# A slot tile's rows two tiles ahead and behind the weights in SyncE's queue, instead of three ahead and in front of them

## The chip, the cores and the metric

The kernel runs on one core of one Trainium2 chip. The metric is the device time of one execution in microseconds (us). Engines are named as in the profile: PE is TensorE, DVE is VectorE, ACT is ScalarE, POOL is GpSimd, SP is SyncE, which only issues DMAs here.

## What is computed

One pre-norm transformer layer on x of shape (4, 2048, 256), float32: causal linear attention with 16 heads of 16, and then a mixture of 8 experts with the top two per token.

```python
x = x + linear_attention(layernorm(x))      # q, k = elu(.) + 1; running sums of k v and of k over the sequence
h = layernorm(x)                            # 8192 tokens
logits = h @ router_w.T                     # 8 experts
top, idx = top_k(logits, 2);  probs = softmax(top)
hmid = gelu(einsum('th,efh->etf', h, w1) + b1)     # 256 -> 512
y    = einsum('etf,ehf->eth', hmid, w2) + b2       # 512 -> 256
out  = x + einsum('eth,te->th', y, combine)        # combine holds probs at the two chosen experts
```

## The kernel before

**Blocks and iterations.** The 8192 tokens are 16 blocks of 512. The main loop has 18 iterations s. Iteration s runs three stages side by side as generators: stage_a of block s (layernorm, projections, the normalizer), stage_b of block s-1 (attention), stage_c of block s-2 (output projection, layernorm, router). Stage_c ends with two small matmuls on PE (`pc`, L596 and L599) that count how many earlier tokens chose each expert. From these DVE works out a slot for each token and choice, and POOL scatters the normalized rows to the DRAM tensor `rows` with eight indirect DMAs (L624). In `rows` each expert has a region of its own, so 256 consecutive slots belong to one expert.

**Slot tiles.** The expert part works on slot tiles of 256 slots. `ROUNDS` says how many full tiles are sure to exist after a number of blocks, whatever the router chose: 5, 4, 8, 8, 8, 8, 8, 22. When a round opens, `plan(r)` finds on DVE which expert and which first row each tile of the round has, and puts them in a small tile `where`. 68 tiles are run in this way; the last few stand under a condition on a count read at run time.

**What one tile does.** `slot_tiles` is a generator over tiles j; each tile takes two steps.

- fetch_rows(j): SP reads the expert and the row number from `where` into registers (L742, L743) and loads the 256 slot rows into a tile `xs` (L747, three buffers).
- fetch_in(j): SP loads the expert's w1 (L759, three buffers). fetch_out(j): w2 and b2 (L767, L771, three buffers).
- turned(j): PE transposes `xs` (`pt_xs`, L780), DVE copies the result to `xT` (L781) and takes the token numbers and weights from the rows.
- hidden(j): PE's first matmul (`ph`, L808), ACT's gelu (L814).
- output(j): PE's second matmul (`py`, L825), DVE's bias and weights (L830, L834); one tile later POOL adds the rows to the output in DRAM (L839).

The first step of tile j holds hidden(j), turned(j+1), fetch_rows(j+3), fetch_in(j+2); the second holds output(j-1), the store of an older tile and fetch_out(j+1).

**What a slot load waits for.** A load of slot rows depends on the scatters that were recorded before it:

```python
after(i, writes + cleared)        # writes: every scatter recorded so far
```

This list also holds scatters of blocks that the tile does not need.

**The order.** SP's queue is issued in the order in which the program is written (`in_order`, a manual schedule of SP alone); an instruction of SP that waits holds all behind it. The order on PE, DVE, ACT and POOL is set when the kernel is built, by a scheduler that goes by the order of recording and by estimates of when operands are ready; each of these engines then runs its list in order.

**Steps per iteration.** Before each iteration the main loop works out how many steps of slot tiles it may take: `limit = 2 * (open_tiles - 3)`, less the steps taken, shared over the iterations until the next round opens. This gives 4, 4, 4 steps in iterations 5 to 7, 8 in each of 8 to 16 and none in 17; the steps left over run after the loop, where no attention work is left. The steps of an iteration are spread between the steps of the three stages.

Of the kernel before, what the change touches and what calls it, by code (L numbers as in the profile page):

```python
# [9 lines left out]
F32 = mybir.dt.float32  # L10
# [6 lines left out]
P = 128  # L17
# [7 lines left out]
def kernel(  # L25
# [44 lines left out]
    E, _, F = w1.shape  # L70
# [10 lines left out]
    NS = ST // P  # L81
# [10 lines left out]
    R = D + 4  # L92
# [5 lines left out]
    moe = ctx.enter_context(tc.tile_pool(name="moe", bufs=2))  # L98
# [12 lines left out]
    def load_x(n: int):  # L111
        b, s0 = blocks[n]
        xt = att.tile([P, NT, D], F32, tag="x", bufs=4, name=f"x_{n}")
        step = P if n == 0 else TB
        for i in range(0, TB, step):
            nc.scalar.dma_start(
                xt[:, i // P : (i + step) // P, :],
                x[b, s0 + i : s0 + i + step, :].rearrange("(t p) d -> p t d", p=P),
            )
        return xt  # L120

    xs = {0: load_x(0)}
# [97 lines left out]
    def ins_of(i):  # L220
        return getattr(i, "ins", i)
# [6 lines left out]
    def after(inst, others):  # L228
        for o in others:
            tc.add_manual_dep(inst, o.name, AFTER, reason="rows written before")  # L230
# [501 lines left out]
    def slot_tiles(todo):  # L732


        state = {}

        def fetch_rows(j):
            r, k = todo[j]
            if r not in plans:
                plans[r] = plan(r)  # L740
            where, te, b1t, behind = plans[r]
            e = nc.sync.value_load(where[0:1, 0, k : k + 1], min_val=0, max_val=E - 1)  # L742
            row = nc.sync.value_load(  # L743
                where[0:1, 1, k : k + 1], min_val=0, max_val=SPARE
            )
            xs_t = moe.tile([P, NS, R], F32, tag="xs", bufs=3, name=f"xs_{r}_{k}")
            i = ins_of(nc.sync.dma_start(  # L747
                xs_t, rows[ds(row, ST), :].rearrange("(a p) d -> p a d", p=P)
            ))
            tc.add_to_no_dep_group("rows", i)  # L750
            after(i, writes + cleared)
            state[j] = {
                "e": e, "xs": xs_t, "bias": b1t[:, k, :], "te": te[:, k : k + 1],
                "behind": None if behind is None else behind[:, k : k + 1],
            }

        def fetch_in(j):
            w1t = moe.tile([P, NCC, F], F32, tag="w1", bufs=3, name=f"w1_{j}")
            nc.sync.dma_start(  # L759
                w1t, w1[ds(state[j]["e"], 1), :, :].rearrange("o (cc p) f -> p (o cc) f", p=P)  # L760
            )
            state[j]["w1"] = w1t

        def fetch_out(j):
            e = state[j]["e"]
            w2t = moe.tile([P, NFC, D], F32, tag="w2", bufs=3, name=f"w2_{j}")
            nc.sync.dma_start(  # L767
                w2t, w2[ds(e, 1), :, :].rearrange("o (fc p) d -> p (o fc) d", p=P)
            )
            b2t = moe.tile([P, D], F32, tag="b2", bufs=3, name=f"b2_{j}")  # L770
            nc.sync.dma_start(b2t, b2[ds(e, 1), :].to_broadcast([P, D]))  # L771
            state[j]["w2"], state[j]["b2"] = w2t, b2t

        def turned(j):
            xs_t = state[j]["xs"]
            xT = moe.tile([P, NCC, ST], F32, tag="xT", name="xT")
            pt = bank([P, NCC, NS, P], "pt_xs")
            for cc in range(NCC):
                for a in range(NS):
                    nc.tensor.transpose(pt[:, cc, a, :], xs_t[:, a, ts(cc, P)], ident)  # L780
            copied = nc.vector.tensor_copy(  # L781
                xT.rearrange("p c s -> p (c s)"), pt.rearrange("p c a s -> p (c a s)")
            )
            state[j]["xs"] = xT

            to = moe.tile([P, NS], U32, tag="to", bufs=10, name=f"to_{j}")
            follow(nc.vector.tensor_copy(to, xs_t[:, :, D]), copied)
            wt = moe.tile([P, NS], F32, tag="wt", bufs=6, name=f"wt_{j}")
            follow(nc.vector.scalar_tensor_tensor(
                wt, xs_t[:, :, D + 3], state[j]["te"], xs_t[:, :, D + 2],  # L790
                ALU.is_equal, ALU.mult,
            ), copied)
            nc.vector.tensor_tensor(wt, wt, xs_t[:, :, D + 1], ALU.add)
            if state[j]["behind"] is not None:
                nc.vector.scalar_tensor_tensor(
                    wt, token[:, 0:NS], state[j]["behind"], wt, ALU.is_ge, ALU.mult
                )
            state[j]["to"], state[j]["wt"] = to, wt

        def hidden(j):  # L800
            xT, w1t, bias = (state[j][key] for key in ("xs", "w1", "bias"))
            hT = moe.tile([P, NFC, ST], F32, tag="hT", name="hT")
            for f2 in range(NFC // 2):
                ph = bank([P, 2, ST], "ph")
                for i in range(2):
                    f = 2 * f2 + i
                    for cc in range(NCC):
                        nc.tensor.matmul(  # L808
                            ph[:, i, :], w1t[:, cc, ts(f, P)], xT[:, cc, :],
                            start=(cc == 0), stop=(cc == NCC - 1),  # L810
                        )
                for i in range(2):
                    f = 2 * f2 + i
                    nc.scalar.activation(  # L814
                        hT[:, f, :], ph[:, i, :], AF.Gelu, bias=bias[:, f : f + 1]
                    )
            state[j]["hT"] = hT
# [33 lines left out]
            return store  # L851

        J = len(todo)
        LEAD = 3
        for j in range(min(LEAD, J)):
            fetch_rows(j)
            if j < LEAD - 1:
                fetch_in(j)
        fetch_out(0)
        yield  # L860
        turned(0)
        wait = []
        for j in range(J + 1):
            if j < J:
                hidden(j)
            if j + 1 < J:
                turned(j + 1)
            if j + LEAD < J:
                fetch_rows(j + LEAD)
            if j + LEAD - 1 < J:  # L870
                fetch_in(j + LEAD - 1)
            if j < J:
                yield
            if j > 0:
                wait.append(output(j - 1))
            while len(wait) > (j < J):
                wait.pop(0)()
            if j + 1 < J:
                fetch_out(j + 1)
            if j < J:  # L880
                yield

# [5 lines left out]
    class Work:  # L888


        def __init__(self, todo):
            self.todo = todo
            self.it = slot_tiles(todo)
            self.steps = 0
# [13 lines left out]
    open_tiles = 0  # L908
    NBLK = len(blocks)
    clear_rows()  # L910
    for s in range(NBLK + 2):
        gens = []
        if s < NBLK:
            gens.append(stage_a(s))
        if 0 <= s - 1 < NBLK:
            gens.append(stage_b(s - 1))
        if s - 2 >= 0:
            gens.append(stage_c(s - 2))

        limit = 2 * (open_tiles - 3)  # L920
        left = max(0, limit - work.steps)

        upto = min([n + 2 for n in begins if n + 2 >= s])
        if s == NBLK + 1:
            left = max(0, left - 2 * HOLD)
        share = -(-left // (upto - s + 1))
        ran = 0
        order = (20, 12, 5)[(s > NBLK - 1) + (s > NBLK)]
        i = 0
        while gens:  # L930
            for it in list(gens):
                if next(it, "end") == "end":
                    gens.remove(it)
                i += 1
                while ran < share and ran * order < i * share:
                    work.step()
                    ran += 1
        while ran < share:
            work.step()
            ran += 1  # L940
        if s - 2 in begins:
            open_tiles += ROUNDS[begins[s - 2]]
# [4 lines left out]
    with ExitStack() as within:  # L947
        for tile_ in todo[LIKELY:]:
            within.enter_context(tc.If(held > tile_[1]))
            for _ in slot_tiles([tile_]):  # L950
                pass
# [44 lines left out]
```

## Time and profile before

| | |
|---|---|
| time of the runs, median (lowest to highest) | 1150.33 us (1149.88 to 1155.89), 3 runs |
| profiled execution: time, span | 1153.22 us, 1151.3 us |
| mean granted PE clock | 0.956 |
| busy: PE, DVE, ACT, POOL | 1035.5, 761.7, 414.7, 389.6 us |
| slot loads (L747): number, KB, median us from issue to landing | 68, 260, 3.3 |
| w1 and w2 loads: number, KB, median us to landing | 136, 512, 5.5 |
| scatters to `rows` (L624): number, mean POOL time | 128, 0.975 us |

The span is from the first to the last instruction of the profiled execution, and its time is a little longer. Busy times of different engines lie beside each other. The profile's timelines give the start of each instruction in us from the span's start, its length, the engine, the line and the tensors; SPq is SP's queue. In brackets stands how long the engine was idle before, and what released it. Iterations 8 to 14 repeat with a period of 62.2 us and hold four slot tiles each.

### The profile page before, as it was taken

To read this page: it belongs to the slowest core of one execution; us is meant where nothing else is said; L and a number is where in the kernel's file an instruction comes from. 1 tells how busy PE (TensorE), PEld (TensorE's weight loads), DVE (VectorE), ACT (ScalarE), POOL (GpSimd) and SP (SyncE) were. 2 spreads that over 40 slices of the span, in tenths; PEclk is the share of its full clock that TensorE was granted. 3 is DMA by queue.
4 is the path that set the end of the run, shared out by engine and by line. 5 is a ranking of instruction groups with operands and counts; after the bars stand their busy time and mean duration, and the time that the engine had idled before them with its cause. 6 is when DMAs were issued, how large, how long until landed. Compare 5 with 4: busy or idle time off the path is not lost.

```text
span 1151.3 us, 23771 instructions
## 1 busy us (share of the span) xinstructions
PE 1035.5 (90%) x8736; PEld 824.5 (72%) x8736; DVE 761.7 (66%) x2534; ACT 414.7 (36%) x824; POOL 389.6 (34%) x302
## 2 busy tenths in 40 slices
PE   5878777797979999999999999999999889999991
PEld 3556556575757687877778777878788678888881
DVE  8778878777677858776777668775777463333330
ACT  3433342434342625353444435362532212222220
POOL 4003123021315253434232433425142353444444
PEclk9889889988989999999999999999999989999996
DMA  6011121441425356372828273736446549888963
GB/s 203 1 38 39 38 75 59 155 138 47 137 58 156 99 132 181 94 221 54 253 45 242 57 213 83 210 81 167 129 104 192 144 131 304 230 231 231 235 151 37
DMA packets 128726, 155.27 MB, mean 135 GB/s; under 512 B 9952, under 2 KB 105952, under 8 KB 128608
## 3 DMA queue, kind: packets, MB, share of 16 engines
q1 hardware_dynamic: 84944, 101.78, 28.0%
q0 software_dynamic: 25728, 34.88, 16.1%
q10 hardware_dynamic: 17936, 17.07, 4.6%
q8 instruction: 70, 1.15, 0.4%
q14 instruction: 48, 0.39, 0.1%
HBM read 108.05 MB, written 45.65 MB: 134 GB/s over the span
## 4 chain that ended last, share of the span: by engine, by line
PE 66%; DVE 27%; DMA 3%; ACT 2%; issue 2%; ACTq 0%; POOL 0%; DVEq 0%; POOLq 0%
PE py L825 20%; PE ph L808 17%; PE pp L338 7%; DVE at L444 6%; PE pn L467 5%; DVE st L266 4%; PE pv L361 3%; PE sc L439 3%; PE pt_xn L259 2%; PE pn L460 2%; DMA out_dram<-y,to 2%; PE pt_xs L780 2%; DVE x L528 2%; DVE z L348 1%; DVE mv L267 1%
## 5 line engine op out<-in xcount | busy, mean ns | idle before, releaser
L839 POOL DMA_INDIRECT out_dram<-y,to x136 | 218.1, 1604 | 451.6 <-DVE y L834 267.5
L825 PE MATMUL py<-w,hT 128*128 128x256 f32 x1088 | 252.1, 385 | 0.0
L808 PE MATMUL ph<-xT,w 128*128 128x256 f32 x1088 | 250.7, 383 | 0.5 <-DVE xT L781 0.4
L814 ACT ACTIVATE hT<-ph,b1t 128x256 f32<-128x256 f32 x272 | 114.3, 471 | 360.3 <-PE ph L808 329.8
L808 PEld LDWEIGHTS ph<-xT,w 128*128 128x128 f32 x1088 | 206.1, 192 | 30.5 <-issue 2.1
L825 PEld LDWEIGHTS py<-w,hT 128*128 128x128 f32 x1088 | 204.3, 193 | 31.3 <-issue 4.3
L444 DVE TENSOR_TENSOR at<-sc,causal 128x512 f32<-128x512 f32 x256 | 159.6, 680 | 11.6 <-PE sc L439 11.6
L624 POOL DMA_INDIRECT rows<-xn,slots x128 | 124.8, 975 | 79.8 <-issue 67.8
L830 DVE TENSOR_TENSOR y<-py,b 128x512 f32<-128x512 f32 x68 | 46.9, 690 | 144.4 <-PE py L825 144.4
L781 DVE COPY xT<-pt_xs 128x512 f32<-128x512 f32 x68 | 46.9, 690 | 115.3 <-PE pt_xs L780 115.3
L316 POOL TENSOR_TENSOR x<-x,bo_bc 128x1024 f32<-128x1024 f32 x16 | 38.4, 2402 | 224.2 <-ACT xn L290 119.2
L430 ACT ACTIVATE qM<-qs,parity 128x256 f32<-128x256 f32 x128 | 57.0, 499 | 92.2 <-DVE qs L409 41.5
L259 PE MATMUL pt_xn<-ident,xn 128*128 128x128 f32 x256 | 46.9, 326 | 44.7 <-DVE xn L295 44.3
L439 PE MATMUL sc<-qM,kT 32*128 32x256 f32 x1024 | 75.4, 406 | 0.7 <-DVE xT L781 0.7
L259 PEld LDWEIGHTS pt_xn<-ident,xn 128*128 128x128 f32 x256 | 35.1, 166 | 56.8 <-issue 35.5
L467 PE MATMUL pn<-at,vpad 128*32 128x128 f32 x2048 | 73.5, 287 | 0.0
L439 PEld LDWEIGHTS sc<-qM,kT 32*128 32x128 f32 x1024 | 47.3, 187 | 26.7 <-issue 17.1
L338 PE MATMUL pp<-xnT,wq_sb 128*128 128x512 f32 x128 | 62.3, 627 | 0.0
L467 PEld LDWEIGHTS pn<-at,vpad 128*32 128x32 f32 x2048 | 55.0, 114 | 8.4 <-issue 0.8
L338 PE MATMUL pp<-xnT,wk_sb 128*128 128x512 f32 x128 | 59.7, 610 | 0.2 <-ACT xnT L260 0.2
L523 PE MATMUL px<-wo_sb,vT 128*128 128x256 f32 x256 | 59.4, 385 | 0.0
L361 PE MATMUL pv<-wv_sb,xnT 128*128 128x256 f32 x256 | 58.5, 382 | 0.0
(151 smaller groups left out, 1339.6 us busy)
## 6 DMA issues: line engine op xcount, KB each, us to landing
w<-in_w_dram SPq DMA_DIRECT2D x136, 512.0 KB, 5.5
xs<-rows SPq DMA_DIRECT2D x68, 260.0 KB, 3.3
b<-in_b_dram SPq DMA_DIRECT2D x68, 128.0 KB, 5.8
out_dram<-x ACTq DMA_DIRECT2D x16, 512.0 KB, 5.2
x<-in_x_dram ACTq DMA_DIRECT2D x15, 512.0 KB, 4.1
rows<-none SPq DMA_DIRECT2D x1, 2340.0 KB, 9.4
out_dram<-y,to POOLq DMA_INDIRECT x136, 4.0
rows<-xn,slots POOLq DMA_INDIRECT x128, 2.5
```

What stands on the lines that cost most here:

```text
L259: nc.tensor.transpose(pt[:, t, :], src[:, t, ts(cc, P)], ident)
L338: nc.tensor.matmul(pp, w[:, cc, ts(m, P)], xnT[:, cc, :], start=(cc == 0), stop=(cc == NCC - 1),)
L361: nc.tensor.matmul(pv[:, j, :], xnT[:, cc, ts(2 * t2 + j, P)], wv_sb[:, cc, :], start=(cc == 0), stop=(cc == NCC - 1),)
L439: nc.tensor.matmul(sc[g][:, m, :, :], kT[part, m, ts(c, P)], qM[part, m, :, :], start=True, stop=True,)
L444: nc.vector.tensor_tensor(at[:, g].rearrange("p m r i -> p (m r) i"), sc[g].rearrange("p m r i -> p (m r) i"), causal.unsqueeze(1).to_broa ...
L467: nc.tensor.matmul(pn[W * g : W * g + W, m, :], vp[:, c, NG * m + g, W * par : W * par + W], at[:, g, m, par, :], start=False, stop=(par = ...
L523: nc.tensor.matmul(px[:, j, :], vT[:, cc, ts(2 * t2 + j, P)], wo_sb[:, cc, :], start=(cc == 0), stop=(cc == NCC - 1),)
L624: s = ins_of(nc.gpsimd.indirect_dma_start(out=rows[:, :], out_offset=bass.IndirectOffsetOnAxis(ap=slots[:, 2 * t + k : 2 * t + k + 1], axi ...
L808: nc.tensor.matmul(ph[:, i, :], w1t[:, cc, ts(f, P)], xT[:, cc, :], start=(cc == 0), stop=(cc == NCC - 1),)
L814: nc.scalar.activation(hT[:, f, :], ph[:, i, :], AF.Gelu, bias=bias[:, f : f + 1])
L825: nc.tensor.matmul(py[:, a, :], hT[:, f, ts(a, P)], w2t[:, f, :], start=(f == 0), stop=(f == NFC - 1),)
L839: i = ins_of(nc.gpsimd.indirect_dma_start(out=out_rows, in_=yt[:, a, :], in_offset=None, compute_op=ALU.add, bounds_check=T - 1, oob_is_er ...
```

## The change

The reading of expert and row number goes into a function of its own, look_up. Tile j's slot rows are now loaded two tiles ahead (LEAD = 2), in the second step and after fetch_out, instead of three tiles ahead in the first step and before fetch_in. The first step of tile j issues look_up(j+2) and fetch_in(j+2), the second fetch_out(j+1) and then fetch_rows(j+2). At the start the order for tile 0 is look-up, w1, w2, b2, slot rows. The step limit becomes 2 * (open_tiles - 2), so that iteration 5 takes 6 steps instead of 4; all later iterations take as many as before, and the part after the loop two fewer.

```diff
-        def fetch_rows(j):
+        def look_up(j):
             r, k = todo[j]
             if r not in plans:
                 plans[r] = plan(r)
...
             row = nc.sync.value_load(
                 where[0:1, 1, k : k + 1], min_val=0, max_val=SPARE
             )
-            xs_t = moe.tile([P, NS, R], F32, tag="xs", bufs=3, name=f"xs_{r}_{k}")
+            state[j] = {
+                "e": e, "row": row, "bias": b1t[:, k, :], "te": te[:, k : k + 1],
+                "behind": None if behind is None else behind[:, k : k + 1],
+            }
+
+        def fetch_rows(j):
+            row = state[j]["row"]
+            xs_t = moe.tile([P, NS, R], F32, tag="xs", bufs=3, name=f"xs_{j}")
             i = ins_of(nc.sync.dma_start(
                 xs_t, rows[ds(row, ST), :].rearrange("(a p) d -> p a d", p=P)
             ))
             tc.add_to_no_dep_group("rows", i)
             after(i, writes + cleared)
-            state[j] = {
-                "e": e, "xs": xs_t, "bias": b1t[:, k, :], "te": te[:, k : k + 1],
-                "behind": None if behind is None else behind[:, k : k + 1],
-            }
+            state[j]["xs"] = xs_t
...
         J = len(todo)
-        LEAD = 3
+
+        LEAD = 2
         for j in range(min(LEAD, J)):
+            look_up(j)
+            fetch_in(j)
+            if j == 0:
+                fetch_out(0)
             fetch_rows(j)
-            if j < LEAD - 1:
-                fetch_in(j)
-        fetch_out(0)
         yield
         turned(0)
         wait = []
...
             if j + 1 < J:
                 turned(j + 1)
             if j + LEAD < J:
-                fetch_rows(j + LEAD)
-            if j + LEAD - 1 < J:
-                fetch_in(j + LEAD - 1)
+                look_up(j + LEAD)
+                fetch_in(j + LEAD)
             if j < J:
                 yield
             if j > 0:
...
             if j + 1 < J:
                 fetch_out(j + 1)
+            if j + LEAD < J:
+                fetch_rows(j + LEAD)
             if j < J:
                 yield
...
-        limit = 2 * (open_tiles - 3)
+        limit = 2 * (open_tiles - 2)
         left = max(0, limit - work.steps)
```

Line numbers move by the change: L747 becomes L754, L759 L763, L767 L771, L780 L784, L808 L812, L825 L829, L839 L843.

## The prediction

> **What bounds the kernel now.** First the page, its part 2: TensorE (PE) is busy in nine tenths or more of nearly every slice from the fourteenth on, at a full granted clock (PEclk). Then the windows view, one window per stage, gives the slack.
>
> ```profile
> PE   5878777797979999999999999999999889999991
> PEclk9889889988989999999999999999999989999996
> ```
> ```profile
> 170.00:240.00 70.00, 56.96 (x632) 43.35 (x632) 56.68 (x216) 28.25 (x55) 16.84 (x14) 0.95 0.29 94
> ...
> 424.00:486.00 62.00, 60.67 (x529) 48.10 (x529) 48.33 (x169) 27.25 (x53) 23.39 (x17) 1.00 0.54 148
> ...
> 925.00:1116.00 191.00, 189.97 (x918) 166.82 (x919) 74.67 (x248) 42.21 (x101) 81.48 (x55) 0.98 0.83 223
> ```
>
> The columns of the second: window, its length, busy us of PE, weight load, DVE, ACT, POOL, then granted clock, DMA share, GB/s. From 424 us on PE idles 1.3 us in a 62 us iteration; before 362 us it idles 8 to 13 us in one. So a wait put in front of PE late is paid in full, and more work put early may be free.
>
> Next, SyncE's (SP) waits. One row stands out:
>
> ```profile
> SPq L747 <- DMA rows<-xn,slots: 437.6, 34, 51.4
> ```
>
> Once per iteration a slot load stands at the head of SP's queue until the scatters of the block routed in that iteration have landed: the load's list of writes holds every scatter recorded so far. In this profile that costs nothing, since that tile is transposed three tiles later. The timelines of POOL, SP and PE show where this wait ends against PE's work in one iteration.
>
> ```profile
> 533.14 1.00 POOL L624 DMA_INDIRECT rows<-xn,slots  x1 [0.30 <-issue]
> ...
> 542.06 0.96 POOL L624 DMA_INDIRECT rows<-xn,slots  x1 [0.30 <-issue]
> ```
> ```profile
> 509.43 0.35 SPq L771 DMA_DIRECT2D b<-in_b_dram  x1
> 544.88 0.37 SPq L747 DMA_DIRECT2D xs<-rows  x1
> ```
> ```profile
> 527.23 0.39 PE L599 MATMUL pc<-sel,ones 128*128 128x64 f32 x2
> ...
> 546.09 0.60 PE L780 MATMUL pt_xs<-ident,xs 128*128 128x128 f32 x4
> ```
>
> Routing ends on PE at 527.2 (pc). Eight scatters follow on POOL; SP is released at 544.88, 17.7 us after pc. PE transposes a slot tile at 546.09.
>
> **The change, part by part.**
>
> *Numbers of instructions.* Per tile SP issues the same two register reads, one slot load, w1, w2 and b2. No engine gains or loses an instruction; all cost is in order and waits.
>
> *The move in SP's queue.* Before: slot load j+3, w1 j+2, then half a tile later w2 and b2 j+1. After: w1 j+2, w2 and b2 j+1, slot load j+2. The weights no longer queue behind the gated load. That gain is worth nothing on the path: in the page's groups PE idles 0.5 us in front of all of L808 and 0.0 in front of all of L825, so no weight comes late now. Cover lost by the slot load: it was recorded four half steps ahead of its transposes, now one.
>
> *The step limit.* 2*(open_tiles - 2) lets one more tile (two steps) run in iteration 5; later iterations have the steps they had. In the built order of the changed kernel each site on PE holds the next tile: at 546.09 stands the tile whose load waits for this iteration's scatters. The gated tiles are the same as before (11, 15, 19 and so on), so release and transposes now meet within an iteration. PE runs in order, so everything after the transposes waits.
>
> *Size of the new wait.* Release R of the gated load (SP timeline) and start T of the transposes at that site (PE timeline), for iterations 8 to 15, which begin at 362 us and are 62.2 us long; landing taken as 3.1 us, the middle of the gated loads' own landings (2.7 to 5.0):
>
> R - T: +1.0, -0.7, -1.2, -0.9, -0.2, -1.0, -1.2, +0.2. Plus 3.1 each: 4.1 + 2.4 + 1.9 + 2.2 + 2.9 + 2.1 + 1.9 + 3.3 = 20.8 us.
>
> Two more, iterations 16 and 17, where attention runs out and less PE work stands between pc and the site:
>
> ```profile
> 905.96 0.60 PE L780 MATMUL pt_xs<-ident,xs 128*128 128x128 f32 x4
> 910.80 0.37 SPq L747 DMA_DIRECT2D xs<-rows  x1
> ...
> 936.07 0.60 PE L780 MATMUL pt_xs<-ident,xs 128*128 128x128 f32 x4
> 941.59 0.37 SPq L747 DMA_DIRECT2D xs<-rows  x1
> ```
>
> 4.8 + 3.1 = 7.9 and 5.5 + 3.1 = 8.6: 16.5 us. DVE works little in the stretch before the site (idle 3.1 and 4.9 us between 534 and 546), so the wait catches up no backlog that would win it back. Waits in front of PE: 37.3 us.
>
> *The clock after the wait.* The trace has gaps of this size already, with their price (same columns as above):
>
> ```profile
> 357.80:360.20 2.40, 0.02 (x3) 0.01 (x1) 2.37 (x5) 0.34 (x1) 1.79 (x3) 1.00 0.24 87
> 360.20:364.00 3.80, 3.77 (x53) 2.98 (x54) 1.57 (x5) 2.08 (x5) 0.59 (x1) 0.66 0.27 70
> ...
> 500.00:506.00 6.00, 4.94 (x43) 3.86 (x42) 5.90 (x40) 4.10 (x9) 0.00 (x0) 1.00 0.59 183
> ```
>
> After the 2.4 us gap the granted clock is 0.66: L467's group took 1.94 us instead of 1.08, L825's 4.39 instead of 3.62, 1.6 us in all. Gaps of 1.9 and 1.5 us did the same (0.65, 0.73; 1.6 and 1.7 us); the 1.0 us gap at 503 did not. The Trainium skill, "TensorE: Matmul & The Clock Gate", Part 1, says that the clock is halved after at least one idle window of about 3.4 us; in the same page's section on oscillation, only gaps above that matter. By the page six or seven of my ten waits cost nothing more (about 6 us for the rest); by the trace each costs 1.65, so 16.5 us. I take the trace, since its gaps are of the size in question.
>
> *Iteration 5, the extra tile.* pc stands at 230.6, release at 247.85, landing 2.8 (median there): the transposes of tile 3 can start at pc + 20. In the new order PE reaches them at pc + 12 (pk, pn, L825 of tile 0, pd, sc, L808 of tile 2). Then pr and two pn groups, about 7 us at the lower clock, and the next L825 at pc + 27; today it starts at 249.1, pc + 18.5. Earlier, PE's 4.8 us gap before 211.5 takes in L808 of tile 0, and pc comes about 1 us sooner. So iteration 5 is some 7 us longer and one tile further. The last stretch loses that tile: 7.35 us there (transposes at 995.17 and 1002.51). Net 0; bounds: -5 if the wait is covered, +4 if DVE falls behind. Iterations 6 and 7 have PE reach their gated tiles only in the following iteration, 10 us or more after release: no cost.
>
> *The last stretch.* The slot load now follows w2, which waits for the L825 two tiles back. From then to its use: L808, transposes, L825, L808 = 10.8 us. It needs about 1.5 us behind w2 and b2, then 3 to 6 us (slot loads there land in 2.7 to 3.5, b2 in up to 5.8). Covered with 3 us left; if that cover went, each us would cost up to 22 us over 22 tiles.
>
> *Sum.* 37.3 + 16.5 + 0 = 54 us, against the profiled execution of 1153.2 us (span 1151.3): 1207. That run was 2.9 us above the median, so 1150.3 + 54, rounded to 1203.
>
> **The rivals.**
>
> *Waits without the clock.* If gaps of 2 us usually straddle what the clock looks at, only the long ones are slowed: 37 + 6 = 43 us, down to 37 with none: 1187 to 1193. For: the page; against: three gaps of three.
>
> *Slower landing.* The release sets free other loads too, and one gated load took 5.0 us. With 5.0 for all ten: 19 us more, 1222. Against: behind the load there now stand only register reads for about 1.3 us, where w1 followed at 0.6.
>
> *Faster: the extra tile fills early slack.* Between 170 and 362 us PE idles 31 us, and the last stretch gets 7.35 us shorter. If the loads land before PE asks, this is all that is left: 1143. It decides when the new waits sum to less than 7.4 us, so the loads would have to be there about 2 us before T in the middle and 8 us earlier at the two late sites. The scatters hang on pc and POOL's own 10 us, which the change leaves alone; so I see no reason for it.
>
> *No change.* The waits could be half covered and the tile gain eat the rest: within 6 us of 1150. Needs both.
>
> **How the numbers follow.** Main case 0.58 (1195 to 1212 its own), waits without the clock 0.18, slower landing 0.12, other slower mixtures 0.03, faster 0.05, no change 0.04. A difference under 0.5% (6 us) is what a measurement of this kernel cannot tell from none. Slower: 0.58 + 0.18 + 0.12 + 0.03 = 0.91. Range 1172 to 1222: the lower end leaves room for landings of 2.7, no lowered clock and 5 us of iteration 5 covered (1150 + 37 - 4 - 5 = 1178) and a little more.
>
> **What would show it.** Right: in the changed profile PE's L784 waits for the DMA xs<-rows, ten or eleven times, 2 to 9 us each, just after a release of SP from the scatters; granted clock near 0.6 for some 4 us behind each; iterations of about 66 us where 62.2 stood; one tile less after the last pc. SP's wait for the scatters stays in the hundreds of us. Wrong: transposes that wait for nothing, the stretch after the last pc slowed per tile, or weights waited for at L812 and L829.

## The result, and the profile after

The changed kernel takes 1182.61 us (median of 6 runs, 1179.29 to 1187.65) against 1150.11 (1147.46 to 1155.89) for the kernel before on the same chip: ratio 1.0279, 95% interval 1.0246 to 1.0311. It is slower, as forecast, and inside the stated range, but by less than the likeliest case said (1203), and below the 1195 to 1212 that the main case gave itself. The profiled execution took 1182.59 us, with a span of 1180.6.

Part 2 of its page, PE's busy tenths and the granted clock in 40 slices:

```profile
PE   4888787877989999999998999999999777999995
PEclk9889889978989999999999999999999878999998
```

PE is still busy in nine tenths of most slices, but there is a dip of three slices where the steady iterations end (slices 32 to 34), with a lower clock. The many small losses do not show at this scale.

The row that the prediction named, in the waits view of the changed kernel (engine, line, waited for: us in total, times, longest):

```profile
PE pt_xs L784 <- DMA xs<-rows: 37.4, 11, 9.1
```

and SP's queue in the same view:

```profile
SPq L771 <- PE py L829: 212.4, 43, 10.6
SPq L754 <- DMA rows<-xn,slots: 201.6, 41, 28.6
```

The kernel before has no such PE row at all; now PE stands eleven times, 37.4 us in sum, in front of its transposes. SP's wait for the scatters fell from 437.6 to 201.6 us, and what vanished there is no gain: SP now first waits for w2's buffer (L771 for the py group that read it, 212.4 us; 69.6 before) and for w1's (L763, 131.2 us; 1.9 before), and comes to the scatters later. The groups of the page show that only the slot rows are late, not the weights (busy us, mean ns, then PE's idle time before the group):

```profile
L829 PE MATMUL py<-w,hT 128*128 128x256 f32 x1088 | 252.1, 385 | 0.0
L812 PE MATMUL ph<-xT,w 128*128 128x256 f32 x1088 | 250.4, 383 | 1.6 <-DVE xT L785 1.6
...
L784 PE MATMUL pt_xs<-ident,xs 128*128 128x128 f32 x272 | 43.3, 284 | 37.4 <-DMA xs<-rows 37.4
```

One of the waits, in iteration 10, in the timelines of POOL, SP and PE of the changed kernel:

```profile
544.88 1.00 POOL L624 DMA_INDIRECT rows<-xn,slots  x1 [0.30 <-issue]
...
553.78 0.96 POOL L624 DMA_INDIRECT rows<-xn,slots  x1 [0.30 <-issue]
```
```profile
556.47 0.37 SPq L754 DMA_DIRECT2D xs<-rows  x1
```
```profile
538.99 0.39 PE L599 MATMUL pc<-sel,ones 128*128 128x64 f32 x2
...
554.29 3.72 PE L812 MATMUL ph<-xT,w 128*128 128x256 f32 x16
559.73 0.63 PE L784 MATMUL pt_xs<-ident,xs 128*128 128x128 f32 x4 [1.72 <-DMA xs<-rows]
```

Routing ends at 538.99, the eighth scatter is issued at 553.78, SP is released at 556.47 (pc + 17.5; it was 17.7), PE is ready at 558.01 (pc + 19.0), and the rows land at 559.73, 3.26 us after the release. PE is 1.5 us behind the release, but a load needs twice that.

Where the time went, stage by stage. A stage is measured by the start of pc in each iteration, before and after: 402.88 and 410.12 in iteration 8, 891.95 and 920.02 in 16, 926.39 and 963.72 in 17; then the end of PE's last group, 1127.1 and 1167.6, and the span, 1151.3 and 1180.6.

| stage | predicted | measured | waits in it |
|---|---|---|---|
| up to iteration 8 (iteration 5, extra tile) | +7 | +7.2 | 6.8 |
| iterations 8 to 15 | 20.8 + 8 x 1.65 = +34.0 | +20.8 | 16.1 |
| iteration 16 | 7.9 + 1.65 = +9.6 | +9.3 | 5.4 |
| iteration 17 to PE's last group, one tile less | 8.6 + 1.65 - 7.35 = +2.9 | +3.1 | 9.1 |
| PE's last group to the end of the span | 0 | -11.1 | |
| sum | +53.5, given as 54 | +29.3 | 37.4 |

Three rows are right within half a us, one of them by luck: in iteration 16 the wait was 5.4 us instead of 7.9, and what came on top of it 3.9 us instead of 1.65, with the granted clock at 0.50 for 10.24 us (third from the end):

```profile
938.01:948.25 10.24, 8.11 (x95) 6.78 (x96) 1.48 (x5) 0.74 (x2) 0.00 (x0) 0.50 0.44 142
```

Two rows are not right: the waits and the lowered clock in the steady iterations, and a stretch at the end that the prediction had left out.

### The profile page after: what moved, and what is told of

Read it like the earlier page. It is cut to its first block, busy times and chain, and to the rows that moved or that the text cites. A ratio compares the mean times of both kernels' runs of the same rounds, so it can differ in the third digit from the quotient of the medians.

```text
span 1180.6 us, 23748 instructions
## 1 busy us (share of the span) xinstructions
PE 1042.4 (88%) x8736; PEld 827.9 (70%) x8736; DVE 759.8 (64%) x2534; ACT 414.3 (35%) x824; POOL 386.6 (33%) x302
## 5 line engine op out<-in xcount | busy, mean ns | idle before, releaser
L843 POOL DMA_INDIRECT out_dram<-y,to x136 | 215.6, 1585 | 479.7 <-DVE y L838 308.2
L829 PE MATMUL py<-w,hT 128*128 128x256 f32 x1088 | 252.1, 385 | 0.0
L812 PE MATMUL ph<-xT,w 128*128 128x256 f32 x1088 | 250.4, 383 | 1.6 <-DVE xT L785 1.6
L812 PEld LDWEIGHTS ph<-xT,w 128*128 128x128 f32 x1088 | 205.8, 191 | 31.6 <-issue 1.9
L829 PEld LDWEIGHTS py<-w,hT 128*128 128x128 f32 x1088 | 204.3, 193 | 31.3 <-issue 4.4
L444 DVE TENSOR_TENSOR at<-sc,causal 128x512 f32<-128x512 f32 x256 | 159.6, 682 | 11.7 <-PE sc L439 11.7
L784 PE MATMUL pt_xs<-ident,xs 128*128 128x128 f32 x272 | 43.3, 284 | 37.4 <-DMA xs<-rows 37.4
L467 PE MATMUL pn<-at,vpad 128*32 128x128 f32 x2048 | 76.2, 294 | 0.0
L784 PEld LDWEIGHTS pt_xs<-ident,xs 128*128 128x128 f32 x272 | 34.5, 146 | 47.7 <-issue 41.8
```

Of the source, the lines that this page charges most:

```text
L444: nc.vector.tensor_tensor(at[:, g].rearrange("p m r i -> p (m r) i"), sc[g].rearrange("p m r i -> p (m r) i"), causal.unsqueeze(1).to_broa ...
L467: nc.tensor.matmul(pn[W * g : W * g + W, m, :], vp[:, c, NG * m + g, W * par : W * par + W], at[:, g, m, par, :], start=False, stop=(par = ...
L812: nc.tensor.matmul(ph[:, i, :], w1t[:, cc, ts(f, P)], xT[:, cc, :], start=(cc == 0), stop=(cc == NCC - 1),)
L829: nc.tensor.matmul(py[:, a, :], hT[:, f, ts(a, P)], w2t[:, f, :], start=(f == 0), stop=(f == NFC - 1),)
L843: i = ins_of(nc.gpsimd.indirect_dma_start(out=out_rows, in_=yt[:, a, :], in_offset=None, compute_op=ALU.add, bounds_check=T - 1, oob_is_er ...
```

## The experiments

The theory: the slot load waits for scatters that its tile does not need; three tiles ahead this is over before PE asks, two tiles ahead it is not. Rivals: the place behind the weights in SP's queue delays the load; the new step limit (the extra tile in iteration 5) shifts the tiles against the scatters. The kernels below change one of these each. Unless said otherwise they start from the changed kernel; ratios are to the kernel before, run beside them on the same chip.

**The list cut down (needed_two_behind).** The load waits only for the scatters that were recorded when its round was planned; these hold all of its rows.

```diff
+                for r in plans:
+                    tc.add_to_no_dep_group(f"late{r}", s)
...
+                needed[r] = list(writes)
...
+            tc.declare_no_dep(i, group=f"late{todo[j][0]}", reason="disjoint rows")
             tc.add_to_no_dep_group("rows", i)
-            after(i, writes + cleared)
+            after(i, needed[todo[j][0]] + cleared)
```

> The changed kernel, but a slot load waits only for the scatters recorded before its round was planned (those whose rows it reads), not for every scatter recorded so far. PE's order of groups is that of the changed kernel. Theory A (the cost is the load's wait for this iteration's scatters, which the shorter lead puts in front of PE): the 11 waits of L784 for xs<-rows (37.4 us) fall below 3 us, SP's wait for scatters from 202 us to under 60, and the time is 1137 to 1148 us, most likely 1143, so below the kernel before by up to 1%: one tile less in the last stretch stays. Rival B (the load lands late because it is issued behind w1, w2 and b2): waits and time stay, 1178 to 1186 us.

Measured: 1135.12 us, ratio 0.9885 (0.9866 to 0.9904), a little below what was expected and below both kernels. PE waits for no slot rows any more, and SP's wait for the scatters is almost gone:

```profile
SPq L758 <- DMA rows<-xn,slots: 5.6, 2, 4.8
```

So the whole loss of the change hangs on that list. With the list cut down, the lead of two, the queue place and the step limit together cost nothing.

**Which part exposes the wait.** The old step limit (limit3_two_behind), the load in front of w1 again but still two ahead (two_in_front), and three ahead with the old limit but behind w2 and b2 (three_behind):

```diff
-        limit = 2 * (open_tiles - 2)
+        limit = 2 * (open_tiles - 3)
```


> The changed kernel with the old step limit 2*(open_tiles - 3), so that no tile is moved to iteration 5; PE's order of groups is that of the kernel before. Theory A: the load that is recorded first behind the scatters is then a tile with a number one lower, and its transposes stand at the same site; ten waits stay (about 2 us in each of iterations 8 to 15, 5 and 9 us in 16 and 17; none in iteration 5), 30 us in all, time 1180 to 1188 us. Rival D (it is the step limit that brings the transposes up to the release): the waits go, 1148 to 1153 us.

```diff
                 look_up(j + LEAD)
+                fetch_rows(j + LEAD)
                 fetch_in(j + LEAD)
...
-            if j + LEAD < J:
-                fetch_rows(j + LEAD)
```


> The changed kernel with the slot load two tiles ahead, but in the first step and in front of w1, as in the kernel before; step limit of the changed kernel, PE's order of groups that of the changed kernel. Theory A: the load at the head of SP's queue is released by the same scatters at the same time and used at the same site, so 11 waits of about 37 us stay, and time is 1178 to 1186 us. Rival B (queue place behind the weights): waits under 5 us, 1140 to 1150 us.

```diff
-        LEAD = 2
+        LEAD = 3
...
-                fetch_in(j + LEAD)
+            if j + LEAD - 1 < J:
+                fetch_in(j + LEAD - 1)
...
-        limit = 2 * (open_tiles - 2)
+        limit = 2 * (open_tiles - 3)
```


> The slot load three tiles ahead with the old step limit, but behind the weights (in the second step, after w2 and b2). PE's order of groups is that of the kernel before. Theory A: the gated load's transposes stand one site (16 us) behind its release, no wait in front of PE, time within 0.4% of the kernel before (1146 to 1155 us). Rival B: a load behind the weights lands late, waits at L784 over 15 us, 1165 us or more.

Measured: 1180.93 us, ratio 1.0267 (1.0250 to 1.0284); 1175.34 us, ratio 1.0251 (1.0202 to 1.0299; one of its four runs took 1188.18); 1150.04 us, ratio 0.9998 (0.9984 to 1.0012). The PE row of the waits view, in this order:

```profile
PE pt_xs L784 <- DMA xs<-rows: 31.1, 10, 8.9
```
```profile
PE pt_xs L784 <- DMA xs<-rows: 23.4, 10, 5.4
```
```profile
PE pt_xs L784 <- DMA xs<-rows: 2.1, 1, 2.1
```

With the old limit the waits of about 2 us in iterations 8 to 15 stand unchanged, and only iteration 5 loses its own; the limit does not bring them. With the load in front of w1 they stand as well, and the waits of iteration 5 and most of that of iteration 17 are gone (9.1 to 1.3 us); so the queue place costs there and nowhere else. Three tiles ahead, behind the weights, one wait of 2.1 us is left and the time is that of the kernel before. The lead does it.

**The cut-down list without the change (needed_three_front).** The same edit in the kernel before.

> The kernel before, with only the slot load's wait cut down to the scatters that its round needs. Theory A: there the wait for later scatters ended before anyone needed the load or the weights behind it, so nothing changes: within 0.4% of the kernel before (1146 to 1153 us), and the gain of the cut-down wait together with two tiles ahead (1135 us) comes from the earlier tile. Rival E (the cut-down wait is worth something by itself, as weights come earlier): 1143 us or less.

Measured: 1141.69 us, ratio 0.9933 (0.9921 to 0.9944). "No change" was wrong: a wait of 437.6 us in SP's queue that held up no engine that the profile shows was still worth 7.4 us. PE's last group ends only 3.4 us earlier (2.5 of them come between iterations 6 and 7); the rest is the end stretch, from PE's last group to the end of the span, 17.2 us instead of 24.2. The next section reads it.

**More scatters (plus_one_scatter, plus_three_scatters).** One, or three, more scatters per block go into a tensor that nobody reads; the load waits for them too (range(3) in the second kernel). This moves the release by a known amount and leaves PE's work alone. The 3.4 us in the expectations is the limit that the prediction cites.

```diff
+        for t in range(1):
+            s = ins_of(nc.gpsimd.indirect_dma_start(
+                out=copy_[:, :],
...
+                in_=xn2[:, t, :], in_offset=None,
+            ))
...
+            writes.append(s)
```


> The changed kernel with one more scatter per block behind the eight (a copy of rows into a tensor that nobody reads), which the slot load also waits for. Its output is that of the reference. Theory A: release of the gated load comes 1.3 us later, so each of the 11 waits of L784's transposes grows by 1.3 us: about 3.3 us in iterations 8 to 15, 51 us in all. Clock: if the chance of a lowered clock grows with the gap, most of the eight are now followed by a slow stretch (1.7 us each) and time is 1202 to 1210 us; if only a gap above 3.4 us counts, few are, and time is 1194 to 1200 us. A rival in which PE is held up by something else than the scatters: waits stay at 37 us.

> The same with three more scatters per block. Theory A: each of the 11 waits grows by 3.8 us, to about 5.8 us in iterations 8 to 15, 79 us in all; every gap is now above 3.4 us, so all are followed by a lowered clock; 1225 to 1240 us. Rival: waits stay at 37 us.

Measured: 1210.92 us, ratio 1.0537 (1.0516 to 1.0557), and 1236.84 us, ratio 1.0762 (1.0739 to 1.0785), two runs each. The PE rows:

```profile
PE pt_xs L795 <- DMA xs<-rows: 50.8, 11, 10.0
```
```profile
PE pt_xs L795 <- DMA xs<-rows: 80.7, 12, 13.0
```

50.8 and 80.7 us against 51 and 79 expected (a twelfth wait, 2.1 us, is new in the second): each scatter adds 1.2 us to every wait, about the 1.27 us by which scatters follow each other on POOL. Waits in front of PE are thus understood to within 2 us in 80. The gaps now have three sizes, which shows what they do to the clock (next section).

**The cut-down list for the late tiles alone (late_needed).** Only tiles 44 to 48, those of iteration 17's wait, get the short list.

```diff
+            only = 44 <= j <= 48
...
-            after(i, writes + cleared)
+            after(i, (needed[todo[j][0]] if only else writes) + cleared)
```


> The changed kernel, in which only the loads of tiles 44 to 48 (the last gated one and those behind it in its round) wait for needed scatters alone. It takes away the last and longest wait, 9.1 us in iteration 17. Theory F (the stretch after the last attention work ends with a chain of stores that lags behind PE; in the changed kernel PE was held up, and the lag was 13 us at the end where the kernel before had 24): PE ends 9 to 11 us earlier, but the time falls by 4 us or less, to 1178 to 1183 us. Rival G (each us of wait costs one): 1171 to 1174 us.

Measured: 1175.99 us, ratio 1.0233 (1.0205 to 1.0262), 6.6 us below the changed kernel, between the two expectations; the intervals of the two ratios overlap, but the profiled executions differ by the same 6.6 us (spans 1174.0 and 1180.6). The wait of 9.1 us is gone and PE's last group ends 11.7 us earlier (1155.85), but the end stretch grows from 13.1 to 18.2 us and takes back 5.1 of it. So what PE wins late is paid out only in part.

**Where the best version's second half comes from.** needed_two_behind gains 14 us and the list alone 7.4. Two kernels with the cut-down list: with the old step limit, and with the load in front of w1.

> The changed kernel with the cut-down list of scatters, and with the old step limit, so without the extra tile in iteration 5. Of the 14 us that the cut-down list with the changed kernel stands below the kernel before, about 7 came with the list alone (three ahead, in front); 6.5 are left. Theory H, the 6.5 are the extra tile in iteration 5, which fills idle PE time there and is missing after the loop: then this kernel is at 1140 to 1143, like the kernel before with the cut-down list (1141.7). Rival I, they come of the lead of two and the queue place (the weights no longer behind a load, fewer loads at once beside the stores): then it stays at 1134 to 1137. In both cases PE waits nowhere for slot rows.

> The changed kernel with the cut-down list and the new step limit, but the slot load in the first step in front of w1. Theory H: the queue place is worth nothing once the load has nothing to wait for; 1133 to 1137, as behind the weights. Rival I: the place counts; in front of w1 it delays the weights by its own issue, 68 times 0.1 us or more, or changes what runs beside the stores: 1139 to 1143.

In these runs the kernel before itself took 1230.25 us, so only the ratios can be read: 1.0008 (0.9990 to 1.0026) and 0.9949 (0.9930 to 0.9969). PE's groups show idle time there that the profile puts to instruction issue (8.2 us in front of py in needed_two_front, none in needed_two_behind); that is a small part of the 80 us, and where the rest comes from stays open. Both were run again:

> The changed kernel with the cut-down list and the old step limit, a second time, since in the first runs the kernel before itself took 1230 us. Theory H: the 6.5 us that the cut-down list with the changed kernel has over the cut-down list alone are the extra tile in iteration 5: 1140 to 1143 here beside a kernel before of 1149. Rival I, they come of the lead of two and the queue place: 1134 to 1137. In the first runs it stood at 1.0008 of the kernel before, on H's side.

> The changed kernel with the cut-down list and the new step limit, slot load in front of w1, a second time for the same reason. Theory H: 1133 to 1137 beside a kernel before of 1149, the queue place being worth nothing once the load has nothing to wait for. Rival I: 1139 to 1143.

Measured: 1140.12 us, ratio 0.9916 (0.9891 to 0.9941), and 1136.55 us, ratio 0.9891 (0.9868 to 0.9915), beside 1151.01 for the kernel before. The load in front of w1 is as good as behind the weights (0.9885): once the load has nothing to wait for, its place is worth nothing. Without the extra tile the kernel is about where the list alone puts it (0.9933; the intervals overlap). With the extra tile it is 3 to 5 us faster; here the intervals overlap, in the first pair of runs they are apart (by 0.6% in the middle). So the extra tile in iteration 5 is probably the larger part of the second half; its size stays rough, and what the lead itself adds is inside the intervals.

## Why the prediction came out right, and where its sum was off

*Order, sites and number: right.* The transposes that follow the scatters of their own iteration wait, eleven of them; SP's wait stays in the hundreds; weights are not late; the last stretch still runs at 7.35 us per tile. Two of the signs named for it did not come: the lowered clock behind each wait (five of the eleven had it), and iterations of about 66 us (six of the eight take the old time, the wait and 0.2 us more). And its reading that SP's wait costs nothing in the kernel before was wrong: needed_three_front puts it at 7.4 us.

*The step limit: the wrong ground.* The prediction's step on the limit said that with it each site on PE holds the next tile. limit3_two_behind has the old limit and the same eight waits. What puts release and use into one iteration is the lead of two; the limit only adds the wait in iteration 5.

*Size of the waits: 37.3 predicted, 37.4 measured, by luck.* The ten waits that were summed took 30.6 us. In iteration 5 PE came at pc + 11.7 (predicted 12) and the rows at pc + 18.5 (20). For iterations 8 to 15 the releases and the site's times of the kernel before were set against each other, R - T from -1.2 to +1.0, in sum 20.8 us with 3.1 of landing. After the change R - T is -1.3 to -1.6 throughout and landing 3.2 to 3.7, in sum 16.1. In iteration 16, R - T was 2.5 instead of 4.8. The eleventh wait, 6.8 us in iteration 5, which the prediction had in its net of that iteration and not in this sum, makes up the difference.

*The clock: the rule from three gaps was too strong.* This is the largest mis-sized term of the sum. The prediction charged 1.65 us for every wait, 13.2 in iterations 8 to 15; those iterations grew by 20.8 - 16.1 = 4.7 us beyond their waits: by 1.8 and 1.7 us in two of them, by 0.2 in each of the six others. So the price of a lowered clock was right, and the number of times wrong. The windows view, 4 us behind some of the waits of 2 us (granted clock third from the end):

```profile
495.60:499.60 4.00, 3.98 (x96) 3.54 (x100) 2.62 (x9) 1.05 (x3) 0.00 (x0) 1.00 1.04 295
559.70:563.70 4.00, 3.95 (x94) 3.54 (x98) 2.56 (x9) 1.00 (x3) 0.00 (x0) 1.00 0.97 310
624.20:628.20 4.00, 3.94 (x93) 3.53 (x97) 2.55 (x9) 0.99 (x3) 0.00 (x0) 1.00 0.92 278
688.70:692.70 4.00, 4.00 (x64) 3.61 (x68) 1.19 (x5) 0.30 (x1) 0.00 (x0) 0.57 0.99 298
...
883.60:887.60 4.00, 4.00 (x68) 3.63 (x72) 1.25 (x5) 0.36 (x1) 0.00 (x0) 0.60 0.99 296
```

The timeline shows the same in the transposes just behind the waits:

```profile
624.24 0.63 PE L784 MATMUL pt_xs<-ident,xs 128*128 128x128 f32 x4 [2.08 <-DMA xs<-rows]
688.67 0.94 PE L784 MATMUL pt_xs<-ident,xs 128*128 128x128 f32 x4 [1.99 <-DMA xs<-rows]
...
883.58 1.09 PE L784 MATMUL pt_xs<-ident,xs 128*128 128x128 f32 x4 [2.27 <-DMA xs<-rows]
```

Gaps of one size, two of eight with a lowered clock. In four kernels (the changed one, limit3_two_behind, two_in_front and late_needed) it was 10 of 32 waits of about 2 us, with a mean of 0.57 to 0.69 over the 4 us behind. With gaps of 3.1 to 3.4 us six of eight had it right behind the wait; here are three of them in plus_one_scatter:

```profile
563.10:567.10 4.00, 4.00 (x72) 3.64 (x72) 1.47 (x5) 0.37 (x1) 0.00 (x0) 0.61 0.99 301
497.50:501.50 4.00, 3.98 (x96) 3.54 (x100) 2.62 (x9) 1.06 (x3) 0.00 (x0) 1.00 0.92 272
430.60:434.60 4.00, 4.00 (x68) 3.59 (x72) 1.28 (x5) 0.37 (x1) 0.00 (x0) 0.57 1.01 304
```

With gaps of 5.3 to 6.0 us all eight had it (0.50 to 0.61); two of them in plus_three_scatters:

```profile
507.80:511.80 4.00, 4.00 (x60) 3.58 (x60) 1.05 (x4) 0.14 (x1) 0.00 (x0) 0.50 1.01 303
578.46:582.46 4.00, 4.00 (x60) 3.60 (x60) 1.05 (x4) 0.13 (x1) 0.00 (x0) 0.53 1.02 297
```

So neither side of the prediction's weighing held. The rule of the Trainium skill ("TensorE: Matmul & The Clock Gate", the section on oscillation), only gaps above 3.4 us, would have given none of these for 2 us; the three gaps of the trace would have given all. The same page says elsewhere (Part 1) that the activity window runs freely, and the traces agree: in every one of them the stretches of granted clock 0.50 begin at multiples of 3.413 us from each other, and all but the last of a trace are one to four times 3.413 us long. Here are two of the 2 us waits, cut at the borders of this grid, each with the window behind it:

```profile
620.57:623.98 3.41, 1.59 (x8) 1.06 (x6) 1.21 (x3) 1.64 (x4) 2.01 (x2) 1.00 0.96 128
623.98:627.40 3.42, 3.14 (x74) 2.85 (x75) 1.75 (x6) 0.37 (x1) 0.00 (x0) 1.00 0.87 237
685.42:688.84 3.42, 1.43 (x8) 0.96 (x7) 0.95 (x1) 1.31 (x4) 1.58 (x1) 1.00 0.98 144
688.84:692.25 3.41, 3.41 (x51) 3.06 (x53) 1.05 (x4) 0.00 (x0) 0.00 (x0) 0.50 1.00 311
```

The wait that ends at 624.24 is the longer one (2.08 us), but a border cuts it into 1.82 and 0.26 us, and the clock stays. The wait that ends at 688.67 (1.99 us) lies whole in one window, and the next window runs at 0.50. Of the 40 waits of 2 and 3 us in iterations 8 to 15 (the four kernels and plus_one_scatter), none of the 23 with less than 1.90 us in a single window lowered the clock, and all 14 with more than 1.93 us did; of the three in between, two did. So it is not the size of a gap alone that decides but where it falls, and a longer gap more often fills enough of one window. The 1.9 us holds for these waits, with dense PE work around them; the prediction's gap of 1.5 us lowered the clock too.

*The end stretch: left out.* The prediction's sum ended at PE's last group. Behind it stands a chain of POOL stores, each pair of which waits for the landing of the pair before. In the kernel before, the first store of each pair in POOL's timeline at the start of the last part:

```profile
940.15 1.62 POOL L839 DMA_INDIRECT out_dram<-y,to  x1 [0.30 <-DVE prod L719]
...
951.00 1.57 POOL L839 DMA_INDIRECT out_dram<-y,to  x1 [7.34 <-DMA out_dram<-y,to]
...
961.53 1.56 POOL L839 DMA_INDIRECT out_dram<-y,to  x1 [7.09 <-DMA out_dram<-y,to]
...
969.88 1.56 POOL L839 DMA_INDIRECT out_dram<-y,to  x1 [4.84 <-DMA out_dram<-y,to]
```

and SP's queue in the same kernel and time:

```profile
941.59 0.37 SPq L747 DMA_DIRECT2D xs<-rows  x1
942.17 0.37 SPq L759 DMA_DIRECT2D w<-in_w_dram  x1
...
945.37 0.37 SPq L747 DMA_DIRECT2D xs<-rows  x1
...
949.00 0.37 SPq L747 DMA_DIRECT2D xs<-rows  x1
```

SP is released from the scatters at 941.59 and issues three tiles' loads in 10 us; the stores beside them come 8.4 to 10.9 us a pair, where a tile of PE takes 7.35. This backlog is carried to the end. In needed_three_front, where SP waits little for the scatters (34.9 us in all), pairs follow after 6.4 to 7.8 us:

```profile
937.58 1.63 POOL L844 DMA_INDIRECT out_dram<-y,to  x1 [0.30 <-issue]
...
945.34 1.60 POOL L844 DMA_INDIRECT out_dram<-y,to  x1 [4.25 <-DVE y L835]
...
951.92 1.56 POOL L844 DMA_INDIRECT out_dram<-y,to  x1 [3.12 <-DMA out_dram<-y,to]
```

In the changed kernel PE stands still for 9.1 us in iteration 17, so the stores come into the last part without a backlog, and the end stretch is 13.1 us instead of 24.2: 11.1 of the 40.5 us that PE ends later are given back. PE's last group, in the kernel before and in the changed one:

```profile
1121.77 5.34 PE L825 MATMUL py<-w,hT 128*128 128x256 f32 x24
```
```profile
1161.79 5.78 PE L829 MATMUL py<-w,hT 128*128 128x256 f32 x26
```

The last stores of the changed kernel wait for their data:

```profile
1158.61 1.56 POOL L843 DMA_INDIRECT out_dram<-y,to  x1 [3.91 <-DVE y L838]
...
1165.51 1.55 POOL L843 DMA_INDIRECT out_dram<-y,to  x1 [3.49 <-DVE y L838]
```

late_needed tests this: with that wait gone the stretch is 18.2 us. two_in_front, with the long list and only 1.3 us of that wait left, shows it more strongly: SP issues three tiles' loads in 10 us from 968.81 on, the stores come 8.5 to 10.8 us a pair there, and the stretch is 25.8 us; PE's last group ends 19.0 us earlier than in the changed kernel, the span only 6.2. That the burst of loads slows the stores fits these runs and needed_three_front, but no run moved the burst alone, so it is not shown.

*The sum.* 54 - 4.7 (waits in the middle) - 8.5 (clock there) - 11.1 (end) = 29.7, against 29.3 us between the two spans. The rival "waits without the clock" (1187 to 1193) was nearest; it, too, lacked the end stretch. "Slower landing" fell: landings were 2.9 to 3.9 us at the waits.

## What to carry to other kernels

A dependency list that names more writers than a load needs cost little while the load was issued early enough (7.4 us here with three tiles of lead), and far more once the lead shrank; cut the list to what the data needs first, then move the load (here 1135 us instead of 1183, with the same lead). A queue wait that no engine shows can still shape what comes after it: here loads came in a burst behind it. And carry a sum through to the last landing: a chain of stores that lags behind the main engine took back part of a delay and part of a gain.

## What the runs showed of the hardware that was not expected

Whether a PE gap of 2 or 3 us lowered the granted clock hung on how much of it fell into one window of a fixed grid of 3.413 us: less than 1.90 us in one window never did (23 waits), more than 1.93 us always did (14). So it was 10 of 32 waits of about 2 us, six of eight of 3.1 to 3.4 us, and all eight of 5.3 to 6.0 us; over the 4 us behind such a gap the mean granted clock was 0.50 to 0.69. Pairs of dependent indirect stores came every 8.4 to 10.9 us beside a burst of loads, and every 6.4 to 7.8 us in the kernel that had none; that the burst is the cause is not shown.
